# Negated upper parts and an adding DMA in place of VectorE's subtraction, for the second layer's weight blocks

## The chip, the cores and the metric

One Trainium2 chip, one core, one launch. The metric is the device time of the launch in microseconds (us). A second, finer source is one profiled execution: its span runs from the first to the last instruction, and the trace behind it says which engine did what and what it waited for. Engines are named as the profile names them: PE (TensorE matmul), DVE (VectorE), ACT (ScalarE), POOL (GpSimd), SP (SyncE, which here only issues DMAs). A q behind an engine's name (SPq) is its queue of DMA issues.

## The reference, cut to what matters

Two layers over x of shape (4, 512, 256), all float32. Layer 0 is a small recurrent mixer, gated; layer 1 is causal attention, gated. Both gates are the same kind of feed-forward network, and the second one's weights are what the change touches:

```python
xn = layernorm(x)
s  = attention(xn)                 # layer 1; a mixer in layer 0
up_gate = xn @ W1.T                # (.., 1024)
up_lin  = xn @ W3.T
hidden  = fwht(silu(up_gate) * up_lin)
g  = silu(hidden @ W2.T)
x  = x + s * g
```

## The kernel before, in words

**Parts of a number.** PE multiplies in a reduced format (float32r), so each float32 matrix goes into PE as two parts: an upper part, the value rounded to that format, and a lower part, the value less its upper part. A product is three matmuls: upper by upper, upper by lower, lower by upper. The helper `split` (line 59) makes the parts: ACT copies with rounding (L61), DVE subtracts (L62). Both lines stand for very many tiles, so the profile is read by tile name.

**Layer 0** works a batch (512 rows) at a time, b = 0 to 3, in `ffn`. Its matmuls are named f_b: `f_3gu` are the up products of batch 3, `f_3dn` the down products. Over eight chunks c of 128 hidden columns it makes two up products (gate and linear), a silu on ACT (L523), their product on DVE (L524), the split of that product (`f_3hh` on ACT, `f_3hl` on DVE), and then, a chunk later, the down products, which take `f_3hh` and `f_3hl` as weights. The up products have three PSUM banks for two per chunk: the second up product of chunk c+1 needs the silu of chunk c to have read its bank, and the first of chunk c+2 needs the gating product L524 of chunk c.

**Layer 1** uses a Strassen-like scheme in `ffn_s`: each 512-wide quarter q of the weights is cut into four blocks of 256 columns, and four sums of blocks are added, seven blocks in all. Blocks and sums are made once, while layer 0 runs batches 2 and 3, by `prep_s(q)` (L322): SP loads four raw blocks into `sraw` (L325), DVE forms four sums in `ssum` (L330 to L333), and both are split into `sp` tiles (three of the raw blocks, 128x768; four sums, 128x1024), which SP stores to DRAM (L342). In layer 1, `load_s` (L345, issue at L350) loads both parts of a quarter (`sw`, 896 KB each) anew for every batch. `sw` tiles share four buffers with layer 0's weights (tag `w13`), so the first ones are loaded while batch 3 of layer 0 finishes with those, each behind its PE wait.

**Side work in layer 0.** `Beside` hands steps of generators to slots between the chunks: for b = 2 the mixer, `prep_s(0)`, the norm of batch 3, `prep_s(1)`, the layer-1 norm of batch 0, `prep_s(2)`; for b = 3 the mixer, the first attention's transposes and splits, `prep_s(3)`. The number beside a generator (4 for `prep_s`) says how many steps it counts for.

**What decides the order.** The kernel is written against a scheduling layer (`TileContext`). It takes the traced program, orders each engine's instructions by its own timing model, gives tiles their buffers, and puts in the semaphore waits. Every engine and every DMA queue then works strictly in the built order: what stands behind a waiting instruction waits too. From layer 0's last products on, PE's order is written out by hand instead. Most tiles of 4 KB per partition, `sraw`, `ssum`, `sp`, and the attention's tiles among them, share ten buffers (tag `t4`), so a tile that is kept longer pushes others to other buffers.

**Names used below.** `ln_3r`, `ln_0r`, `mr`, `ssr`: row scales, raised to the power -1/2 by POOL (L261, L277, L724), its only regular work. `xn_3`: the normed batch 3 of layer 0. `mrb`: mean and scale rows of layer 1's norm, broadcast through DRAM by SP (L445, L447). `osb`: the mixer's output. `tsum`, `tb`, `xf`, `xg`: layer 1's activations for batch 0, made from two transposes. `tq`, `v`, `sc`: products of the attention.

Of the kernel before, what the change touches and what calls it, by code (L numbers as in the profile page):

```python
# [11 lines left out]
F32 = mybir.dt.float32  # L12
# [3 lines left out]
F32R = mybir.dt.float32r  # L16
AF = mybir.ActivationFunctionType
ALU = mybir.AluOpType
# [3 lines left out]
P = 128  # L22
D = 256
# [12 lines left out]
def kernel(ctx: ExitStack, tc: tile.TileContext, a: dict, out: bass.AP):  # L36
    nc = tc.nc
# [6 lines left out]
    def t4(name, shape, dt=F32):  # L44
        return act.tile(shape, dt, tag="t4", name=name, bufs=10)
# [10 lines left out]
    def psum(name, shape, tag="ms", bufs=3):  # L56
        return ps.tile(shape, F32, tag=tag, name=name, bufs=bufs)

    def split(src, hi, lo, engine=nc.vector):

        h = nc.scalar.copy(hi, src)  # L61
        return h, engine.tensor_tensor(lo, src, hi.bitcast(F32), ALU.subtract)  # L62
# [14 lines left out]
    def transpose(*args):  # L77
        return in_line(nc.tensor.transpose, *args)
# [94 lines left out]
    def w2_tile(name):  # L173
        return wp.tile([P, NH, D], F32R, tag="w2", name=name, bufs=4)

    def w2_tiles(layer):
        return w2_tile(f"w2h_{layer}"), w2_tile(f"w2l_{layer}")
# [73 lines left out]
    def moments(name, x, mr):  # L251

        st = act.tile([P, NT, 6], F32, tag="stats", name=f"{name}st", bufs=4)
        mv = act.tile([P, NT, 2], F32, tag="mv", name=f"{name}mv", bufs=4)
        for t in range(NT):
            nc.vector.bn_stats(st[:, t, :], x[:, t, :])
        for t in range(NT):
            nc.vector.bn_aggr(mv[:, t, :], st[:, t, :])
        nc.vector.tensor_copy(mr[:, 0, :], mv[:, :, 0])
        first["moments"] = nc.vector.tensor_scalar(mr[:, 1, :], mv[:, :, 1], LN_EPS, None, ALU.add)  # L260
        nc.gpsimd.tensor_tensor(mr[:, 1, :], mr[:, 1, :], mhalf, ALU.pow)  # L261

    def layernorm(name, x, y, groups=(NT,)):

        t0 = 0
        for i, n in enumerate(groups):
            ts_ = range(t0, t0 + n)
            st = act.tile([P, NT, 6], F32, tag="stats", name=f"{name}st{i}", bufs=4)
            mv = act.tile([P, NT, 2], F32, tag="mv", name=f"{name}mv{i}", bufs=4)
            r = small(f"{name}r{i}")  # L270
            for t in ts_:
                nc.vector.bn_stats(st[:, t, :], x[:, t, :])
            for t in ts_:
                nc.vector.bn_aggr(mv[:, t, :], st[:, t, :])
            rs = r[:, t0 : t0 + n]
            nc.vector.tensor_scalar(rs, mv[:, t0 : t0 + n, 1], LN_EPS, None, ALU.add)
            nc.gpsimd.tensor_tensor(rs, rs, mhalf[:, :n], ALU.pow)  # L277
            for t in ts_:
                ins = nc.vector.tensor_scalar(
                    y[:, t, :], x[:, t, :], mv[:, t, 0:1], r[:, t : t + 1], ALU.subtract, ALU.mult  # L280
                )
            t0 += n
        return ins

    def transpose_half(name, y, k):
        o = psum(f"{name}tp{k}", [P, S])
        for t in range(NT):
            transpose(o[:, sl(t)], y[:, t, sl(k)], ident)
        return o
# [14 lines left out]
    def xt_pair(name):  # L304

        both = act.tile([P, 2, 2, S], F32R, tag="xt", name=name, bufs=2)
        return both[:, 0], both[:, 1]
# [14 lines left out]
    def prep_s(q):  # L322

        raw = t4(f"sraw{q}", [P, 4, D])
        nc.sync.dma_start(raw, a["w13_1"][q])  # L325
        yield
        sums = t4(f"ssum{q}", [P, 4, D])
        a11, a12, a22, a21 = (raw[:, i, :] for i in range(4))
        s1, s2, s3, s4 = (sums[:, i, :] for i in range(4))
        nc.vector.tensor_tensor(s1, a21, a22, ALU.add)  # L330
        nc.vector.tensor_tensor(s3, a11, a21, ALU.subtract)
        nc.vector.tensor_tensor(s2, s1, a11, ALU.subtract)
        nc.vector.tensor_tensor(s4, a12, s2, ALU.subtract)  # L333
        yield
        sdram[q] = there = [
            dram.tile([P, 7, D], F32, tag=f"s{i}", name=f"s{i}_{q}", bufs=4) for i in range(2)
        ]
        for at, n, src in ((0, 3, raw), (3, 4, sums)):
            parts = [t4(f"sp{at}_{i}_{q}", [P, n, D], F32R) for i in range(2)]
            split(src[:, :n, :], *parts)  # L340
            for i in range(2):
                nc.sync.dma_start(there[i][:, at : at + n, :], parts[i].bitcast(F32))  # L342
            yield

    def load_s(q, n):  # L345
        parts = [
            wp.tile([P, 7, D], F32R, tag="w13", name=f"sw{i}_{n}_{q}", bufs=4) for i in range(2)
        ]
        for i in range(2):
            nc.sync.dma_start(parts[i].bitcast(F32), sdram[q][i])  # L350
        return parts
# [75 lines left out]
    def norm(layer, b):  # L427
        xn = act.tile([P, NT, D], F32, tag="xn", name=f"xn{layer}_{b}", bufs=3)
        xns[layer, b] = xn
        with after(first["gate"] if b > 1 - layer else None):  # L430
            first["scaled"] = layernorm(f"ln{layer}_{b}", xs[b], xn)
        yield
        if layer:


            mr = act.tile([P, 2, NT], F32, tag="mr", name=f"mr{b}", bufs=2)
            moments(f"ln2_{b}", xn, mr)
            yield
            o = psum(f"mrp{b}", [2 * NT, P], **DN[b == 0])
            transpose(o, mr.rearrange("p a t -> p (a t)"), ident)  # L440
            rows = act.tile([2 * NT, P], F32, tag="rows", name=f"rows{b}", bufs=1)
            with after(first["table"] if b else None):
                nc.scalar.copy(rows, o)
            there = dram.tile([2 * NT, P], F32, tag="rows", name=f"there{b}")
            nc.sync.dma_start(there, rows)  # L445
            mrb = t4(f"mrb{b}", [P, 2, S])
            nc.sync.dma_start(  # L447
                mrb, there.rearrange("(a t) p -> a (t p)", a=2).unsqueeze(0).to_broadcast([P, 2, S])
            )
            mrs[b] = mrb  # L450
            yield
            return
        hi, lo = xTs[0, b] = xt_pair(f"xt0_{b}")
        for k in range(2):
            o = transpose_half(f"xt0_{b}", xn, k)
            split(o, hi[:, k, :], lo[:, k, :])
            yield

    def after(ins):
        return tc.issue_after(ins.ins) if ins else nullcontext()  # L460
# [441 lines left out]
    def run(f, *args):  # L902
        return lambda: f(*args)

    def call(f, *args):
        f(*args)
        yield


    NORM, MIXER, W2P = 3, 3, 12  # L910
# [80 lines left out]
    for b in range(B):  # L991
        tasks = []
        if b == 0:
            prep = prep_first()
            next(prep)
            tasks.append((prep, 11))
        if b:
            tasks.append((call(gate_all, f"g0_{b - 1}", dn, xns[0, b - 1], xs[b - 1]), 1))
        tasks.append((mixer(b), MIXER))
        if b + 1 < B:  # L1000
            if b:
                load_x(b + 1)
            if b == 2:
                tasks.append((prep_s(0), 4))
            tasks.append((norm(0, b + 1), NORM))
        if b == 0:
            early = w2_tile("early0"), w2_tile("early1")
            spare = [
                [early[i][:, 2 * c : 2 * c + 2, :].rearrange("p a d -> p (a d)") for i in range(2)]
                for c in range(NH // 2)  # L1010
            ]
        if b == 1:
            raw2_1 = load_w2(1)
            w2_1 = w2_tiles(1)
            tasks.append((prep_w2(1, raw2_1, w2_1, t4), W2P))
            tasks.append((prep_second(), 5))
        if b == 2:
            tasks += [(prep_s(1), 4), (norm(1, 0), NORM), (prep_s(2), 4)]
        if b == 3:
            atts = [Attention(0)]  # L1020
            at = atts[0]
            parts = run(at.xt_half, 0), run(at.xt_half, 1), at.xt, at.scaled, at.split_sums
            tasks += [(call(f), 1) for f in parts]
            norms = {1: norm(1, 1)}
            tasks.append((prep_s(3), 4))
        bg = Beside(*tasks)
        if b == 0:
            dn = ffn("f0_0", xTs[0, 0], w13, w2, bg.slot, NH, spare, parts=2, behind=True)
        else:
            tail = [run(atts[0].tq, j) for j in range(2)] if b + 1 == B else []  # L1030
            dn = ffn(f"f0_{b}", xTs[0, b], w13, w2, bg.slot, tail=tail)
        bg.finish()
# [148 lines left out]
```

## Time and profile before

| | |
|---|---|
| median of 3 runs | 362.86 us (362.65 to 363.22) |
| the profiled execution's own time | 362.72 us |
| its span | 360.9 us |
| granted TensorE clock | 1.00 |
| DVE, ACT, POOL busy | 286.1, 197.5, 19.0 us (79%, 55%, 5%) |
| DMA of the kernel's own queues | q1 39.8%, q10 0.2% of 16 engines' span |

Busy time is the time in which an engine worked on an instruction of the program. A PE row of many matmuls is pipelined: a matmul of 512 columns is listed with some 0.39 us, but in an unbroken run the next starts 0.23 us later (0.12 us after one of 256 columns), so starts are compared, not durations. The same holds in a smaller way for DVE and ACT: a DVE operation over 512 columns is listed with 0.68 us and the next starts 0.60 us later.

### The profile page before, as it was taken

The page shows a single profiled execution, that of the slowest core. Times are in us where ns is not written, and L with a number is a line of the kernel's source. Part 1 is how long each engine was busy: PE and PEld are TensorE (multiplying, and loading weights), DVE is VectorE, ACT ScalarE, POOL GpSimd, SP SyncE. Part 2 cuts the span into 40 slices and gives each one's busy share as a digit, 9 for nine tenths or more (in the row PEclk, how much of TensorE's full clock was granted, in tenths as well). Part 3 has the DMA queues.
Part 4 walks back from the last instruction along what each step waited for, and adds up shares of the span by engine and source line. Part 5 has one row for each costly group of instructions (what it writes and reads, how often), then busy time and mean ns, then how long its engine had stood idle before and what let it go on. Part 6 is the DMA issues. An engine that isn't in the chain of part 4 may idle for free.

```text
span 360.9 us, 6262 instructions
## 1 busy us (share of the span) xinstructions
PE 354.3 (98%) x2469; PEld 327.9 (91%) x2469; DVE 286.1 (79%) x592; ACT 197.5 (55%) x372; POOL 19.0 (5%) x22
## 2 busy tenths in 40 slices
PE   8999999999999999999999999999999999999995
PEld 6878999888988898888999999999999999999995
DVE  6897868996679938898987957989679888568646
ACT  4665436274454335465467655576555676446443
POOL 1000201100011000100100001100011000000000
PEclk9999999999999999999999999999999999999999
DMA  7935000301063217637257135661554635345401
GB/s 228 346 108 186 3 0 2 116 0 60 0 196 155 118 52 236 237 130 254 85 206 261 49 157 205 223 226 79 203 205 152 215 162 203 136 149 193 194 2 58
DMA packets 16284, 52.25 MB, mean 145 GB/s; under 512 B 1632, under 2 KB 7936, under 8 KB 16256
## 3 DMA queue, kind: packets, MB, share of 16 engines
q1 hardware_dynamic: 15968, 51.60, 39.8%
q8 instruction: 19, 0.31, 0.3%
q10 hardware_dynamic: 288, 0.26, 0.2%
q14 instruction: 9, 0.07, 0.1%
HBM read 42.40 MB, written 9.45 MB: 144 GB/s over the span
## 4 chain that ended last, share of the span: by engine, by line
PE 78%; DVE 16%; ACT 2%; DMA 1%; issue 1%; POOL 1%; DVEq 0%; SPq 0%; ACTq 0%
PE f_0gu L70 6%; PE f_1gu L70 6%; PE f_0dn L70 5%; PE f_2dn L70 5%; PE f_3dn L70 5%; PE f_1dn L70 5%; PE f_3gu L70 5%; PE pv L70 4%; PE f_2gu L70 3%; PE tq L70 2%; PE o L70 2%; PE v L70 2%; PE sc L70 2%; PE warm L70 2%; DMA sraw<-in_w 1%; DVE sp L62 1%
## 5 line engine op out<-in xcount | busy, mean ns | idle before, releaser
L70 PE MATMUL f_3gu<-xt,w 128*128 128x512 f32 x96 | 25.6, 397 | 0.0
L70 PE MATMUL f_0gu<-xt,w 128*128 128x512 f32 (+1 forms) x108 | 24.9, 382 | 0.0
L70 PE MATMUL f_1gu<-xt,w 128*128 128x512 f32 x96 | 24.8, 395 | 0.0
L70 PE MATMUL f_2gu<-xt,w 128*128 128x512 f32 x96 | 24.6, 395 | 0.0
L70 PEld LDWEIGHTS f_0gu<-xt,w 128*128 128x128 f32 x108 | 18.6, 188 | 4.4 <-issue 1.0
L70 PEld LDWEIGHTS f_2gu<-xt,w 128*128 128x128 f32 x96 | 17.2, 188 | 3.2
L70 PEld LDWEIGHTS f_1gu<-xt,w 128*128 128x128 f32 x96 | 17.1, 188 | 3.2
L70 PEld LDWEIGHTS f_3gu<-xt,w 128*128 128x128 f32 x96 | 17.1, 188 | 2.9
L61 ACT CAST f_1hh<-f_1h 128x512 fp32r<-128x512 f32 x16 | 10.0, 623 | 16.7 <-DVE f_1h L524 13.6
L70 PE MATMUL f_1dn<-w2l,f_1hh 128*128 128x256 f32 x64 | 17.8, 282 | 0.0
L70 PE MATMUL f_2dn<-w2h,f_2hh 128*128 128x256 f32 x64 | 17.8, 283 | 0.0
L70 PE MATMUL f_1dn<-w2h,f_1hh 128*128 128x256 f32 x64 | 17.8, 281 | 0.0
L70 PE MATMUL f_2dn<-w2l,f_2hh 128*128 128x256 f32 x64 | 17.7, 283 | 0.0
L70 PE MATMUL f_3dn<-w2l,f_3hh 128*128 128x256 f32 x64 | 17.7, 282 | 0.0
L70 PE MATMUL f_3dn<-w2h,f_3hh 128*128 128x256 f32 x64 | 17.7, 281 | 0.0
L70 PE MATMUL f_3dn<-w2h,f_3hl 128*128 128x256 f32 x64 | 17.0, 283 | 0.4 <-DVE f_3hl L62 0.4
L70 PE MATMUL f_1dn<-w2h,f_1hl 128*128 128x256 f32 x64 | 17.1, 283 | 0.0
L70 PE MATMUL f_2dn<-w2h,f_2hl 128*128 128x256 f32 x64 | 16.8, 283 | 0.2 <-DVE f_2hl L62 0.2
L61 ACT CAST f_2hh<-f_2h 128x512 fp32r<-128x512 f32 x16 | 9.9, 621 | 12.4 <-DVE f_2h L524 9.1
L61 ACT CAST f_3hh<-f_3h 128x512 fp32r<-128x512 f32 (+1 forms) x17 | 10.1, 596 | 11.3 <-DVE f_3h L524 7.1
L62 DVE TENSOR_TENSOR f_2hl<-f_2h,f_2hh 128x512 fp32r<-128x512 f32 x16 | 10.9, 682 | 3.9 <-ACT f_2hh L61 3.8
L70 PE MATMUL f_0dn<-w2h,f_0hl 128*128 128x256 f32 x48 | 13.7, 284 | 0.1
(480 smaller groups left out, 1139.4 us busy)
## 6 DMA issues: line engine op xcount, KB each, us to landing
sw<-s SPq DMA_DIRECT2D x32, 896.0 KB, 5.5
s<-sp SPq DMA_DIRECT2D x8, 512.0 KB, 4.1
s<-sp SPq DMA_DIRECT2D x8, 384.0 KB, 2.5
w2raw<-in_w SPq DMA_DIRECT2D x4, 512.0 KB, 5.9
sraw<-in_w SPq DMA_DIRECT2D x4, 512.0 KB, 4.4
mrb<-there SPq DMA_DIRECT2D x4, 512.0 KB, 3.9
w13raw<-in_w SPq DMA_DIRECT2D x3, 512.0 KB, 6.6
x<-in_x SPq DMA_DIRECT2D x3, 512.0 KB, 3.4
```

The source lines that it names most:

```text
L61: h = nc.scalar.copy(hi, src)
L62: return h, engine.tensor_tensor(lo, src, hi.bitcast(F32), ALU.subtract)
L70: ins = call(*args, **kwargs)
```

## The change

Step by step, for the raw blocks and for the sums of each quarter: ACT makes the negated upper part (a multiplication by -1 with rounding) and then the upper part; a DMA issued by POOL adds the negated upper part onto the float32 source in place, which leaves the lower part there; SP stores the upper part as before, and the source itself as the lower part. The subtraction on DVE is gone. `prep_s` has one step more, and counts as 5.

```diff
+
         for at, n, src in ((0, 3, raw), (3, 4, sums)):
-            parts = [t4(f"sp{at}_{i}_{q}", [P, n, D], F32R) for i in range(2)]
-            split(src[:, :n, :], *parts)
-            for i in range(2):
-                nc.sync.dma_start(there[i][:, at : at + n, :], parts[i].bitcast(F32))
+            src = src[:, :n, :]
+            hi, neg = (t4(f"sp{at}_{i}_{q}", [P, n, D], F32R) for i in range(2))
+            nc.scalar.mul(neg, src, -1.0)
+            nc.scalar.copy(hi, src)
+            nc.gpsimd.dma_start(src, neg.bitcast(F32), accum_op=ALU.add)
+            nc.sync.dma_start(there[0][:, at : at + n, :], hi.bitcast(F32))
             yield
+            nc.sync.dma_start(there[1][:, at : at + n, :], src)
+        yield
...
-                tasks.append((prep_s(0), 4))
+                tasks.append((prep_s(0), 5))
...
-            tasks += [(prep_s(1), 4), (norm(1, 0), NORM), (prep_s(2), 4)]
+            tasks += [(prep_s(1), 5), (norm(1, 0), NORM), (prep_s(2), 5)]
...
-            tasks.append((prep_s(3), 4))
+            tasks.append((prep_s(3), 5))
```

Since the layer orders the program anew, other instructions of batches 2 and 3 change places too; the listing of both built programs shows which.

## The prediction

> **What bounds the kernel now.** I read the page's first part, then what PE waited for, then PE's and DVE's order of time around each wait, then DVE's and ACT's rows of the tiles that change.
>
> ```profile
> PE 354.3 (98%) x2469; PEld 327.9 (91%) x2469; DVE 286.1 (79%) x592; ACT 197.5 (55%) x372; POOL 19.0 (5%) x22
> ```
>
> PE is the bound, with 6.6 us of idle span. What it waited for, by the waits view:
>
> ```profile
> PE warm L70 <- DVE zr L921: 1.4, 1, 1.4
> PE f_3dn L70 <- DVE f_3hl L62: 0.4, 1, 0.4
> PE f_2dn L70 <- DVE f_2hl L62: 0.2, 1, 0.2
> ```
>
> (Us in total, times, longest.) The first is the start. The other two lie in the stages that the change touches, one each in batches 2 and 3. PE's order of time shows their price:
>
> ```profile
> 112.44 1.55 PE L70 MATMUL f_2gu<-xt,w 128*128 128x512 f32 x6
> 114.22 0.38 PE L70 MATMUL f_2dn<-w2h,f_2hl 128*128 128x256 f32 x1 [0.22 <-DVE f_2hl L62]
> 114.44 0.28 PE L70 MATMUL f_2dn<-w2h,f_2hh 128*128 128x256 f32 x1
> ...
> 170.57 0.28 PE L70 MATMUL f_3dn<-w2l,f_3hh 128*128 128x256 f32 x1
> 171.27 0.39 PE L70 MATMUL f_3dn<-w2h,f_3hl 128*128 128x256 f32 x1 [0.42 <-DVE f_3hl L62]
> 171.50 0.28 PE L70 MATMUL f_3dn<-w2h,f_3hh 128*128 128x256 f32 x1
> ```
>
> Six up matmuls take 1.39 us from start to start, so the product of 114.22 was due at 113.83: 0.39 lost, and 0.10 more since its successor follows after 0.22 instead of 0.12. The second was due at 170.69: 0.58 and 0.11. Together **1.18 us**; elsewhere between 94 and 171 us no PE row shows idle time. DVE at those two places:
>
> ```profile
> 112.51 0.92 DVE L62 TENSOR_TENSOR sp<-sraw,sp 128x768 fp32r<-128x768 f32 x1
> ...
> 113.51 0.66 DVE L62 TENSOR_TENSOR f_2hl<-f_2h,f_2hh 128x512 fp32r<-128x512 f32 x1
> ...
> 168.68 1.20 DVE L62 TENSOR_TENSOR sp<-ssum,sp 128x1024 fp32r<-128x1024 f32 x1
> 169.81 0.68 DVE L62 TENSOR_TENSOR tql<-tq,tqh 128x512 fp32r<-128x512 f32 x1
> ...
> 170.56 0.65 DVE L62 TENSOR_TENSOR f_3hl<-f_3h,f_3hh 128x512 fp32r<-128x512 f32 x1
> ```
>
> In both, a subtraction of `sp` stands ahead of the late `f_2hl` or `f_3hl`. The change removes exactly these.
>
> **What goes.** Eight DVE subtractions: 4 x 0.95 + 4 x 1.22 = 8.7 us (rows of `sp`). Beside PE's 98% all of it but the two waits is hidden, so the ceiling of the gain is 1.18 us. Without the 1.13 us that `sp` occupies, the second `f_3hl` starts near 169.4 and ends before 170.2, ahead of 170.69; its upper part is ready at 168.1. The first is freed likewise: in the built order nothing of `prep_s` stands between the row sums of `ln_3` and `f_2hl` but one block sum (0.34), and my sum of DVE's starts puts `f_2hl`'s end at 113.0.
>
> **What comes on ACT.** Eight copies with a factor of -1. A factor costs ACT nothing visible: 0.60 us for `wqkh` (factor, 128x512) against 0.58 for `tqh` (copy). So 4 x 0.84 + 4 x 1.05 = 7.6 us, on an engine at 55%. Behind them on ACT are silu and upper part of the next chunks. In batch 2 the tightest is the silu of chunk 2: it ends near 106.9, and PE needs it at 108.24. In batch 3 both copies of `sraw` go ahead of chunk 1's silu (139.3, wanted at 142.4). Cover: over 1 us; price here nothing. Without that cover each further copy would cost PE up to its 0.74 to 0.96 us.
>
> **What comes on POOL.** Eight DMA issues, which the trace does not have. Queued behind them are `ln_3r`, `ln_0r`, `mr` and `ssr`. An adding DMA waits for ACT's copy of the same tile and DVE's last block sum. `ln_3r` stands behind the third one (ready near 112.3); `xn_3` is then done near 116.8, and PE's transposes want it near 119. For an issue I take SPq's 0.3 to 0.6 us as the lower bound, and as the upper one POOL's own 1.0 to 1.4 us for an operation; even two of the latter fit into the 2.2 us. Nothing.
>
> **How long an adding DMA takes.** No row shows it. Below: a plain copy of the same 512 KB (`s<-sp`), 4.1 us median. Above: twice the longest landing of `s<-sp`, 6.6, so 13.2 us. The page *Collectives: The Full Stack*, section "The bandwidth ceiling", says that an add in the DMA path reads two sources and so runs at half a copy's rate. The row alone would give 4, the rule 8; I take **8 us**, since the stretch from 140 to 148 us already moves 263 to 422 GB/s and the adds fall into it.
>
> A second rule speaks against the change: *SBUF — State Buffer*, section "SBUF: two separate sides", warns that POOL cannot write a DMA's descriptors while DVE runs an operation that takes both port pairs, as a float32 copy in SBUF does; its example grows from 620 to 3100 ns. The nearest such rows here, `xn<-x` (TENSOR_SCALAR, 128x256), start 0.33 us apart, as two-input additions do (0.34): no double rate, hence no sign of that mode. By the row nothing is added; by the rule's example 2.5 us are, and 8 becomes 10.5.
>
> **What comes on SP.** The store of the lower part now waits for the add, and SP keeps its order. Behind the one of `ssum` for q = 2 stand the load of `sw`'s lower half and of `sraw` for q = 3. ACT makes that negated part near 141.5 and the upper part near 142.5, so with 8 us the add lands near 150.6. The lower half of `sw` may not go before PE is done with its buffer, now 149.19, so SP is held some 1.4 us. `sraw` for q = 3 is issued near 151.4 instead of 158.48, as it moved ahead of another `sw`; with its 5.4 us it lands near 156.8. DVE's block sums for q = 3 moved forward too, behind chunk 4's gating product, near 157.9. So nothing waits, with **1 us of slack**: that is the point at which the adds begin to cost. The `sw` behind `sraw` q = 3's store would be issued near 168 instead of 165.5, and is wanted at 182. The longer hold on the ten buffers costs nothing more, as no reuse in the built order comes that close.
>
> **What is moved.** With DVE's subtractions gone the order is made anew, and in batch 3 DVE gets more to do before chunk 4's gating product. Now `ssr` of the mixer is at 147.59 and that product ends at 154.88. In the built order, between the same two: three 256-column operations (0.34 apart), four of `osb` (1.6), seven of 512 (0.60), two of 1024 (1.13), then the product (0.60 + 0.69 for the two gating ones): 1.0 + 1.6 + 4.2 + 2.3 + 1.3 = 10.4 us. `ssr` itself comes at about 147.5, as ACT's extra copies for q = 2 (0.74 + 0.96) use what is now waiting time. So the product ends near 157.9. PE wants it for the up product of chunk 6: now at 157.87, then 157.38, the first gap being closed. **A new wait of 0.5 us, with the slower start 0.6.** Both of its bounds: below, nothing (my sums of starts are good to about 0.6); above, 1.2.
>
> **Sum**, against the profiled execution's own 362.72 us: -0.49 - 0.69 + 0.6 = -0.6, 362.1. The median of the runs is 0.14 above that execution: **362.3 us**.
>
> **The rivals.**
> 1. *Gaps closed, one new wait on DVE* (as above): 362.3, between 361.7 and 362.9. Chance 0.42.
> 2. *The new wait doesn't arise*, DVE and PE fitting as the scheduler intended: 362.86 - 1.18 = 361.7. For it: PE has 3 us of slack at that product now. Against: the sum of 10.4 us. Chance 0.21.
> 3. *The add holds SP.* Slower. From 9 us of an add on, `sraw` for q = 3 lands late, and DVE waits in its block sums with chunk 4's lower part and chunk 5's gating product queued behind. At 13 us it lands at 161.9, 4 us late; PE has some 0.8 us of slack there (chunk 4's lower part ready near 160.4, wanted near 161.2). That is +3.2 on top of rival 1: 365.5. For it: DMA traffic in that stretch, two reads per add, a wait on SP that did not exist. Against: 13 is my upper bound. Chance 0.27.
> 4. *The gaps only move*: freed DVE time goes to row statistics that were ordered forward, and PE meets the same wait elsewhere: 362.9. Against: DVE loses 3% of its work. Chance 0.10.
>
> **How the numbers follow.** About 0.2% (0.73 us, so 362.13 and 363.59) is what a measurement tells from no change. Faster by more: 0.21 of rival 2 and 0.12 of rival 1, 0.33. Within: 0.28 of rival 1, 0.07 of rival 4, 0.35. Slower: 0.27 of rival 3, the rest of 1 and 4, 0.32. The range leaves out the slowest third of rival 3 and little below 361.5: 361.5 to 366.0. The likeliest case's own is 361.7 to 362.9.
>
> **What would show it.** Right: no PE wait for `f_2hl` and `f_3hl` near 114 and 170, DVE busy near 277 us, ACT near 205, and one PE wait of about half a microsecond for `f_3h` L524's successor near 157. Rival 3: DVE idle for the DMA of `sraw` near 158, and an issue to landing of the adds above 9 us. Rival 2: PE idle down by 1.2 us with no new wait. Wrong altogether: POOL rows of several microseconds per DMA issue, with `xn_3` late, or waits in layer 1, which I take to be unchanged.

## The result, and the profile after

The changed kernel takes **363.97 us** (median of 13 runs, 363.35 to 364.89) against 362.92 (362.65 to 363.22) of the kernel before beside it: ratio 1.0027, 95% interval 1.0019 to 1.0036. It is slower by 1.05 us where I forecast 0.6 us less. The profiled execution took 363.47 us with a span of 361.3.

The page's first part, the row of the engines:

```profile
PE 354.0 (98%) x2469; PEld 328.2 (91%) x2469; DVE 278.5 (77%) x584; ACT 204.1 (56%) x380; POOL 25.9 (7%) x30
```

The work went where it was meant to go: DVE is down by 7.6 us, ACT up by 6.6, POOL up by 6.9 for eight issues. What PE waited for (us in total, times, longest):

```profile
PE warm L70 <- DVE zr L926: 1.5, 1, 1.5
PE f_3dn L70 <- ACT f_3hh L61: 1.1, 1, 1.1
PE f_0dn L70 <- DVE f_0hl L62: 0.2, 1, 0.2
```

Both old waits, behind `f_2hl` and `f_3hl`, are gone. In their place stands one behind an upper part, which ACT makes. PE's order of time there:

```profile
157.35 0.28 PE L70 MATMUL f_3dn<-w2h,f_3hl 128*128 128x256 f32 x1
157.69 1.68 PE L70 MATMUL f_3gu<-xt,w 128*128 128x512 f32 x6
160.44 0.38 PE L70 MATMUL f_3dn<-w2h,f_3hh 128*128 128x256 f32 x1 [1.08 <-ACT f_3hh L61]
160.66 0.28 PE L70 MATMUL f_3dn<-w2l,f_3hh 128*128 128x256 f32 x1
```

From start to start: 157.69 comes 0.34 after its predecessor instead of 0.12 and its own six are 0.10 slow, 0.32 together: DVE's gating product, which I had at 0.6. Then 160.44 comes 2.75 after 157.69 instead of 1.39, or 1.25 after the slow start is taken off, and 0.10 more follow: **1.35 us behind `f_3hh`**, which is in no step of my sum. So PE's starts say -1.18 + 0.32 + 1.35 = +0.49. The span grew by 0.4, and the time outside the span from 1.82 to 2.17 us (see the end).

What made `f_3hh` late is read from the chain of work that ends with it (start, us, what):

```profile
142.97 7.75 DMA ssum<-sp
...
150.77 0.32 SPq L347
...
151.15 0.42 SPq L355
...
151.62 6.05 DMA sraw<-in_w
...
157.78 0.85 ACT sp L342
158.63 0.72 ACT sp L343
159.35 0.52 ACT xgh L61
159.87 0.53 ACT f_3hh L61
...
160.44 0.74 PE f_3dn L70 x4
```

Read downwards: the add of `ssum` q=2 lands; SP may then store the lower part, load a `sw` and, third, load the raw blocks of q=3; ACT, which had been free since 156.15 (its row shows 1.63 us idle before the copy), waits for them with the negated copy at its head; two copies and `xgh` later it makes `f_3hh` of chunk 4, for which PE has been waiting.

**Theory 1:** the add holds the last chunk's load, and that load holds ACT, with `f_3hh` queued behind. **Rivals:** the new order and ACT's extra 7.6 us cost the time whatever the load does; or the adds cost it wherever they run, by traffic, by their number or outside the span.

### The profile page after: what moved, and what is told of

The parts are those of the page before. It is cut to its first block, busy times and chain, and to the rows that moved or that the text cites. A ratio compares the mean times of both kernels' runs of the same rounds, so it can differ in the third digit from the quotient of the medians.

```text
span 361.3 us, 6295 instructions
## 1 busy us (share of the span) xinstructions
PE 354.0 (98%) x2469; PEld 328.2 (91%) x2469; DVE 278.5 (77%) x584; ACT 204.1 (56%) x380; POOL 25.9 (7%) x30
## 4 chain that ended last, share of the span: by engine, by line
PE 78%; DVE 11%; DMA 6%; ACT 3%; issue 1%; POOL 1%; SPq 0%; DVEq 0%; ACTq 0%
PE f_0gu L70 6%; PE f_1gu L70 6%; PE f_2gu L70 6%; PE f_0dn L70 5%; PE f_2dn L70 5%; PE f_1dn L70 5%; PE f_3dn L70 4%; PE pv L70 4%; PE tq L70 3%; DMA sraw<-in_w 3%; PE o L70 2%; PE v L70 2%; DMA ssum<-sp 2%; PE sc L70 2%; PE f_3gu L70 2%; PE warm L70 2%
## 5 line engine op out<-in xcount | busy, mean ns | idle before, releaser
L70 PE MATMUL f_3gu<-xt,w 128*128 128x512 f32 x96 | 24.7, 397 | 0.1
L62 DVE TENSOR_TENSOR f_3hl<-f_3h,f_3hh 128x512 fp32r<-128x512 f32 (+1 forms) x17 | 11.1, 656 | 5.1 <-ACT f_3hh L61 5.0
```

Source lines behind the costliest of these rows:

```text
L70: ins = call(*args, **kwargs)
```

## The experiments

In each group the kernel before ran on the same chip: 362.83 us for the first four, 363.17 for the next four, 363.05 for the last three. I tell them in the order of the argument.

**No add at all** (2nd group)

```diff
-            nc.gpsimd.dma_start(src, neg.bitcast(F32), accum_op=ALU.add)
```

> The changed kernel without the adding DMAs: the subtraction is left out, and what is stored as the lower part is the source itself; ACT's negated copies, all loads and all stores stay. It has the order of ACT of the changed kernel around `f_3hh` of chunk 4, but no load, store or buffer waits for an add. Theory 1 (what costs is the time of the adds, which hold buffers and so the load): `sraw` of q=3 is issued by 146, ACT doesn't wait for it, DVE's short wait of 0.3 us may stay, and the time is 361.8 to 362.4. Rival (the moved order on ACT and DVE and ACT's 7.6 us more of work cost the time): the wait behind `f_3hh` of about 1 us stays and the time is 363.5 to 364.

Measured: 361.49 us, ratio 0.9955 (0.9942 to 0.9969), some 0.3 below theory 1's range. ACT's order of time:

```profile
154.98 0.85 ACT L342 ACTIVATE sp<-sraw 128x768 fp32r<-128x768 f32 x1 [2.37 <-DMA sraw<-in_w]
155.74 0.82 ACT L343 CAST sp<-sraw 128x768 fp32r<-128x768 f32 x1
156.86 0.82 ACT L774 ACTIVATE xg<-xf,gb 128x512 f32<-128x512 f32 x1 [0.30 <-DVE xf L772]
157.58 0.60 ACT L61 CAST f_3hh<-f_3h 128x512 fp32r<-128x512 f32 x1
```

The two copies stand ahead of `f_3hh` as in the changed kernel, and ACT even waits longer for the load; but the load was issued at 149.57 and landed 2.8 us earlier, so `f_3hh` starts at 157.58 instead of 159.77, and PE loses 0.12 us there. I expected the issue by 146; `sw`, in front of it on SP, waits for PE until 149.20, adds or not. With the load on time this order of ACT costs next to nothing, so the order alone is not the cost: the loss needs the late load.

**Chunk q=2 the old way** (2nd group)

```diff
+        if not (q != 2):
+            for at, n, src in ((0, 3, raw), (3, 4, sums)):
+                parts = [t4(f"sp{at}_{i}_{q}", [P, n, D], F32R) for i in range(2)]
+                split(src[:, :n, :], *parts)
...
+            return
```

> The changed kernel with chunk q=2 alone split the old way (DVE subtracts, its lower part is a tile of its own), adds for q=0, 1 and 3. Theory 1 (the load of `sraw` q=3 waited for the buffer that the add of `ssum` q=2 held): the load is issued near 145 instead of 151.6, ACT's wait at it and PE's 1.35 us behind `f_3hh` go; one of the two old waits (behind an `sp` subtraction of q=2, about 0.5) may come back: 362.4 to 363.0. Rival (q=3's own adds, or the number of adds, cost the time): 363.6 to 364.

Measured: 361.48 us, ratio 0.9954 (0.9941 to 0.9966), better than expected, as neither old wait came back: the load is issued at 149.72 (not near 145, for `sw` again stands in front of it until 149.35), and PE waits for nothing but the start:

```profile
PE warm L70 <- DVE zr L934: 1.5, 1, 1.5
```

Six of the eight adds are still there, those of q=3 among them, and cost nothing that shows. But this edit moves two things: the new build also has `f_3hh` of chunk 4 ahead of the two copies on ACT.

```profile
155.78 0.61 ACT L61 CAST f_3hh<-f_3h 128x512 fp32r<-128x512 f32 x1
157.30 0.83 ACT L350 ACTIVATE sp<-sraw 128x768 fp32r<-128x768 f32 x1
```

So the earlier load and the changed order are not told apart here; the run without adds, which keeps the copies in front, does that.

**Chunk q=3 the old way** (3rd group; the edit of the last run with another condition)

```diff
-        if not (q != 2):
+        if not (q < 3):
```

> The changed kernel with the last chunk (q=3) split the old way, adds for q=0, 1 and 2: the counterpart to the run with q=2 undone. Theory 1 (the harm comes from q=2's add, ahead of the load, and from ACT's copies of q=3's raw blocks ahead of `f_3hh` of chunk 4, not from q=3's own adds): the load is issued near 151.6 as in the changed kernel and lands near 157; ACT waits for it, with one copy of 0.73 us fewer behind the wait, so PE still loses 0.4 to 1.2 us near 160: 363.0 to 363.8. Rival (q=3's own adds cost the time): the wait goes and the time is as with q=2 undone, 361.4 to 361.8.

Measured: 362.98 us, ratio 0.9994 (0.9986 to 1.0003), just below theory 1's range, and not to be told from the kernel before. PE's wait is there though q=3 has no add:

```profile
160.10 0.39 PE L70 MATMUL f_3dn<-w2h,f_3hh 128*128 128x256 f32 x1 [0.53 <-ACT f_3hh L61]
```

The load was issued at 151.78 and ACT's one copy started at 158.18; PE lost 0.80 us. The two runs together clear q=3's own adds: without them the wait stays, and with them it is absent once q=2's adds are gone.

**The changed kernel again** (3rd group, nothing edited)

> The changed kernel once more, unaltered, beside the two others on the same chip. Theory 1: 363.8 to 364.4 us, with the wait of 1.0 to 1.5 us behind `f_3hh` near 160 and the same time outside the span, 2.1 to 2.2 us, since that has been the same in every run of one program so far. If the loss were of the chip of the first measurement, it would be within 0.2 us of the kernel before.

Measured: 364.44 us, ratio 1.0048 (1.0029 to 1.0066), a shade above theory 1's range. In its profile the load took 6.54 us, ACT's copy started at 158.33, and PE lost 1.94 us. Against the first profile the copy came 0.55 later and the loss was 0.59 larger; against the run before this one there is one copy more (0.75 us) and the start is 0.15 later, PE's up products begin 0.26 earlier (157.66 against 157.92), and the loss is 1.14 larger. The loss follows the start of the copies nearly one to one. It fits that the first 13 runs of this kernel spread over 1.5 us where those of the kernel before spread over 0.6: here a DMA's landing is on PE's path.

One thing is not explained by the landing. Three of the eight runs took 365.83 to 366.35 us, and their mean granted TensorE clock was 0.995; the other five took 363.59 to 364.70 at 0.998 to 1.000, and none of the first 13 runs was below 0.997. A mean of 0.995 over 364 us is 1.8 us of full clock, about what sets the three apart (an estimate). No trace shows one of these three; two traces below show the clock at 0.50 for some microseconds behind a wait of PE.

**Is it SP's order or the buffer?** (3rd group)

```diff
-            nc.sync.dma_start(there[1][:, at : at + n, :], src)
+            eng = nc.gpsimd if q == 2 and at else nc.sync
+            eng.dma_start(there[1][:, at : at + n, :], src)
```

> The changed kernel with one store moved to another queue: the lower part of `ssum` q=2, which waits for the add of that tile and stood on SP ahead of the last chunk's raw load, is issued by POOL, behind the add itself. SP isn't held any more; the load's buffer, though, is still the tile that this add reads. It asks which of the two holds the load. Theory 1a (SP's order alone): the load of `sraw` q=3 is issued at 149.6 as in the kernel without adds, lands by 155.2, and PE's 1.35 us behind `f_3hh` shrink to 0.2: 362.6 to 363.0 us. Theory 1b (the buffer holds it as well): the load is issued when the add has landed, 150.5 to 151, lands near 156.3 to 157, PE loses 0.5 to 1.1 us, and the time is 363.2 to 363.8.

Measured: 363.97 us, ratio 1.0037 (1.0022 to 1.0052). SP's order of time, what the load waited for, and ACT's order of time:

```profile
149.36 0.32 SPq L356 DMA_DIRECT2D sw<-s  x1
150.97 0.33 SPq L325 DMA_DIRECT2D sraw<-in_w  x1
```

```profile
SPq L325 <- DMA ssum<-sp: 1.3, 1, 1.3
```

```profile
158.24 0.85 ACT L342 ACTIVATE sp<-sraw 128x768 fp32r<-128x768 f32 x1 [1.86 <-DMA s<-ssum]
```

SP is past `sw` at 149.68 and free, yet the load starts at 150.97, when the add has landed: in the built program its buffer is the negated tile that this add reads. Theory 1b holds for the issue. The time is over its 363.8, for a reason that I had not foreseen: the negated copy of q=3 takes the buffer of the tile that is being stored, and the store now ends last (6.9 us), so PE lost 1.59 us. Freeing one queue moved the wait to another buffer.

**Each add twice** (1st group; each of half the negated part)

```diff
-            nc.scalar.mul(neg, src, -1.0)
+            nc.scalar.mul(neg, src, -0.5)
...
-            nc.gpsimd.dma_start(src, neg.bitcast(F32), accum_op=ALU.add)
+            for _ in range(2):
+                nc.gpsimd.dma_start(src, neg.bitcast(F32), accum_op=ALU.add)
```

> The changed kernel, with each adding DMA made twice, each time of half the negated part (so the sum is the same), one behind the other: what waits for the sum waits for two adds, some 5 to 7 us longer. Theory 1 (the add of `ssum` q=2 frees the buffer late, SP issues the load of q=3's raw blocks behind it, ACT waits for that load): the load is issued near 157 to 158 and lands near 163, ACT's wait grows from 1.6 to some 7 us, PE's wait behind `f_3hh` from 1.35 to 6 to 7 us, and the time is 369 to 371. Rival (the latency of the add is not what counts, but the order on ACT and DVE): the time stays within 1 us of 364.0.

Measured: 373.37 us, ratio 1.0290 (1.0275 to 1.0304), 2 us above theory 1's range. PE's waits, and the chain:

```profile
PE f_3dn L70 <- DVE f_3hl L62: 5.4, 1, 5.4
PE f_3gu L70 <- DVE f_3h L530: 2.3, 2, 1.4
```

```profile
144.19 5.24 DMA sraw<-sp
...
149.72 6.29 DMA sraw<-sp
156.02 4.78 DMA s<-sraw
160.82 6.05 DMA sraw<-in_w
...
166.99 0.43 DVE ssum L330
167.42 0.34 DVE ssum L331
167.75 0.61 DVE f_3hl L62
168.41 2.07 PE f_3dn L70 x8
```

The late load is again what PE waits for in the end, but it holds another reader. In this build ACT made `f_3hh` of chunk 4 at 160.87, before it stood at the load (5.40 us idle); DVE stood at the load with its block sums, and `f_3hl` behind them kept PE waiting. The issue missed, too: 160.82 instead of 157 to 158, since here the load waited for the store behind the two adds as well. The rival, that the latency does not count, is out.

The wait of 5.4 us is no longer than forecast. What goes beyond the range is 2.3 us at gating products, earlier in the batch, and a slower PE behind the long wait:

```profile
168.41 0.58 PE L70 MATMUL f_3dn<-w2h,f_3hl 128*128 128x256 f32 x1 [5.39 <-DVE f_3hl L62]
...
170.28 4.58 PE L70 MATMUL f_3gu<-xt,w 128*128 128x512 f32 x12
174.70 0.28 PE L70 MATMUL f_3dn<-w2h,f_3hh 128*128 128x256 f32 x1
```

Twelve up matmuls take 4.42 us from start to start instead of 2.8, and the granted clock was 0.50 between 168 and 172 us, where the changed kernel has 1.00 throughout. From 168.41 to 174.70 that is 6.29 us for what takes 3.7 at the usual spacing: 2.6 us lost.

**The load early** (2nd group)

```diff
         if b == 3:
+            last_s = prep_s(3)
+            next(last_s)
...
-            tasks.append((prep_s(3), 5))
+            tasks.append((last_s, 4))
```

> The changed kernel, with the load of the last chunk's raw blocks (`sraw` of q=3) asked for at the start of batch 3, ahead of that batch's other tasks, so that it takes a buffer that no late adding DMA holds. The adds, the copies and their number stay. Theory 1 (the 1.35 us are ACT at a load that the add of `ssum` q=2 had held up): the load is issued before 145 and landed before 152, ACT's wait and PE's wait behind `f_3hh` near 160 go, and the time is 362.4 to 362.9 us. Rival from the first runs (ten buffers and longer holds: take the wait away in one place and another instruction waits for an add's buffer): a new wait behind an `sp` DMA of 1 us or more appears later, and the time is 363.7 or more.

Measured: 361.69 us, ratio 0.9960 (0.9948 to 0.9973), a little better than expected. The load is issued at 139.98; PE waits only at the start (1.5 us). All eight adds are in place, and 512 KB take 7.0 us by the median, longer than in the changed kernel (6.5). So the adds as such are not the cost. As with q=2 undone, `f_3hh` of chunk 4 (155.37) now stands ahead of the copies of q=3 (157.60) on ACT, so this run too moves the load and the order together.

**The negated copy later** (1st group)

```diff
-            nc.scalar.mul(neg, src, -1.0)
+            with after(first["hh"] if q == 3 and at == 0 else None):
+                nc.scalar.mul(neg, src, -1.0)
```

> The changed kernel, with one order of ACT altered: the negated copy of the last chunk's raw blocks (the `sp` from `sraw` of q=3) must come behind the `f_hh` that stands newest when it is recorded, so ACT no longer waits for that load with `f_3hh` of chunk 4 behind it. Theory 1 (the loss is ACT standing at a late load, 1.35 us of PE behind `f_3hh`): that wait of `f_3dn` at 160.4 goes, DVE's short wait of 0.3 us stays, and the time is 362.6 us, some 1.3 below the changed kernel and 0.3 below the kernel before. Rival (the adding DMAs slow things wherever they run, the wait is only where it shows): the wait moves to another product of the same batch, and the time stays within 0.3 us of 364.0.

Measured: 366.98 us, ratio 1.0106 (1.0083 to 1.0129). The half of theory 1 that it asks about held: PE's `f_3dn` at 159.68 comes 1.51 us after its predecessor, no wait, though the load is as late as in the changed kernel (issued at 152.19; DVE waits for it until 158.59). So it takes both, a late load and ACT's copies in front of `f_3hh`. But the copy ended up behind the last chunks, at 164.02 instead of 157.78, so q=3's add was issued at 165.88, took 9.57 us, and DVE's order of time says who stood behind it:

```profile
176.00 1.29 DVE L62 TENSOR_TENSOR tql<-tq,tqh 128x512 fp32r<-128x512 f32 x2 [4.90 <-DMA sraw<-sp]
```

```profile
PE f_0gu0g L70 <- DVE f_0h L657: 1.7, 1, 1.7
PE v L70 <- DVE tql L62: 1.5, 1, 1.5
```

(The second fence shows PE's waits.) `tql` had to wait for the add to let a buffer go. The expectation of 362.6 was wrong by 4.4 us: I had moved the add along with the copy and not asked who needs its tiles. The rival's "the wait moves" is what happened, only into another stage and larger. Here, too, the clock fell behind a wait: 0.50 between 186 and 188 us. Of the six runs, the two with a mean clock of 0.997 and 1.000 took 365.3 us, the four with 0.995 took 366.6 to 367.8.

**The gain without an add** (1st group; the splits of the kernel before, held behind the newest `f_hl`)

```diff
-            split(src[:, :n, :], *parts)
+            with after(first["hl"]):
+                split(src[:, :n, :], *parts)
```

> The kernel before, no adding DMA: only the splits of the weight blocks (the rounded copies of ACT and the subtractions of DVE) must come behind the `f_hl` that is newest when they are recorded. Theory 1 (the two waits of PE in the kernel before, 0.49 and 0.69 us, are the place of the `sp` subtractions ahead of `f_2hl` and `f_3hl` on DVE): both waits go without taking the subtractions off DVE, and the time is 361.7 to 362.3. Rival (the load of DVE matters, not the place): the waits move to other products, and the time is 362.7 to 363.2.

Measured: 361.82 us, ratio 0.9972 (0.9962 to 0.9983). Both old waits are gone with DVE still at 285.7 us. So they were a matter of place, not of DVE's load. New ones of 0.6 and 0.2 us (`f_0gu1z` and `f_0gu2z` behind DVE's `f_0h`) take back part of the 1.18.

**The subtractions on POOL** (2nd group)

```diff
-            split(src[:, :n, :], *parts)
+            split(src[:, :n, :], *parts, engine=nc.gpsimd)
```

> The kernel before with the eight `sp` subtractions moved from DVE to POOL as they are: no adding DMA, no negated copy, the lower part a tile of its own. It asks what taking the subtractions off DVE is worth without the adds' latency and holds. Theory 1: both old waits of PE (0.49 and 0.69 us) go, the 128x768 and 128x1024 subtractions take POOL 2 to 4 us each with slack enough, and the time is 361.7 to 362.3. Rival (POOL and DVE get in each other's way, so DVE's instructions beside POOL's grow longer; or the stores come too late): 362.8 to 364.

Measured: 363.39 us, ratio 1.0007 (0.9998 to 1.0015): the rival. A POOL row and a DVE row of the same moment:

```profile
165.54 2.40 POOL L62 TENSOR_TENSOR sp<-ssum,sp 128x1024 fp32r<-128x1024 f32 x1 [3.66 <-ACT sp L61]
```

```profile
166.01 2.47 DVE L62 TENSOR_TENSOR f_3hl<-f_3h,f_3hh 128x512 fp32r<-128x512 f32 x1 [1.04 <-ACT f_3hh L61]
```

An `f_3hl` that takes 0.68 us elsewhere takes 2.47: it ends when POOL's subtraction has ended (167.94) and its own time is over. One `xn` of 0.41 us took 2.50 in the same way. The wait behind `f_3hl` is gone, but in batch 2 PE now waits for gating products that DVE makes late:

```profile
PE f_2gu L70 <- DVE f_2h L524: 0.4, 2, 0.3
```

The work left DVE and came back as stalls: the spans are 361.0 to 361.7 us against 361.1 to 361.7 of the kernel before.

**One adding DMA that nobody waits for** (1st group, kernel before)

```diff
+    idle = [small(f"idle{i}") for i in range(2)]
+    for t in idle:
+        nc.gpsimd.memset(t, 0.0)
+    nc.gpsimd.dma_start(idle[0], idle[1], accum_op=ALU.add)
```

> The kernel before, with two small tiles (128x4) set to zero and one adding DMA between them on POOL's queue near the start, which nobody waits for. Theory 1 says that 0.35 us of the loss lies outside the span and comes with any use of POOL's software queue: the execution's time less its span goes from 1.82 to about 2.17 us, the span stays within 0.2 of 360.9, and the time is 363.2 to 363.3. Rival (the 0.35 us is the end of the changed program, or chance): time less span stays at 1.8 and the time at 362.9.

Measured: 362.55 us, ratio 0.9991 (0.9983 to 0.9999), time outside the span 1.74 to 1.85 us. My explanation of the 0.35 us falls.

## Why the prediction was wrong, step by step

- **The ceiling of 1.18 us** was right: both waits went, and kernels that add no other wait gain it in the profile (span 359.7 with q=2 undone, 360.9 before).
- **The add's 8 us** were right: 7.75 us for the one that mattered, landing at 150.7 against 150.6; by the median 6.5 us for 512 KB against 3.8 for the plain copy `s<-sp` of the same kernel, 1.7 times. How much of that is the adding and how much POOL's queue is not shown: the one plain store that POOL issued (in "Is it SP's order or the buffer?") took 6.9 us, beside the load. POOL's issues took 0.86 to 1.04 us, with no sign in these rows of the 2.5 us that I had worked out from the example in the Trainium skill, page *SBUF — State Buffer*, section "SBUF: two separate sides".
- **POOL's queue** cost nothing, as I said: `ln_3r` at 114.22, no wait of PE near 119.
- **The new DVE wait** was 0.32 us, not 0.6, within its bounds.
- **The step that failed** is the one on SP: "So nothing waits, with 1 us of slack". The issue was as forecast (151.62 against 151.4), the load took 6.05 us instead of 5.4, and it landed 0.9 us later than I said. That alone was inside the slack. But the slack was that of the wrong waiter: I had asked when DVE's block sums come (157.9; they did wait 0.17), and not ACT's negated copy, which the built order has at ACT's head from 156.15, with `xgh`, `f_3hh` and a silu behind it. With the load at 156.8 as forecast, PE would still have lost 1.35 - 0.9, some 0.45 us (an estimate).
- **ACT's "price here nothing"** failed with it: I checked the copies of q=1 and q=2 against the silu behind them, and not those of q=3 against `f_3hh`. The added copy of q=3 is 0.75 us of the 1.35.
- **"The longer hold on the ten buffers costs nothing more"** was wrong: the buffer of `sraw` q=3 is one that the add still reads, and in three experiments a tile waited for an add or a store behind it.
- **Rival 3** had the mechanism, "the add holds SP", but its threshold ("from 9 us of an add on"), its waiter (DVE) and its price (+3.2) were off. It decided at less than 8 us, by ACT. With each add made twice, DVE is the waiter as the rival has it: 5.4 us behind its block sums.

With -1.18 + 0.32 + 1.35 in place of my -1.18 + 0.6, the sum on the profiled execution is 363.2; the rest to 363.47 lies outside the span. Since the landing varies, the typical loss is larger: the second profile of the same program shows 1.94.

Two versions beat both kernels by repairing that one load: q=2 split the old way (361.48 us) and the load early (361.69), some 0.4 to 0.5% below the kernel before. Simply moving the subtractions, with no add, gets 361.82; that one ran in another group, and the intervals overlap in part. The first two ran side by side with spans of 359.6 to 359.8 us each; the 0.2 us between them lies outside the span. So I don't rank the three.

## What to carry to other kernels

When an operation with a long latency replaces a short one, follow its landing through everything that is issued or allocated behind it, and for the last load in that line list *every* engine that reads it, with what is queued behind each reader: the slack is that of the earliest reader. A tile that a DMA still reads is a held buffer, and a cure that delays the DMA moves the hold. If a wait is due to an instruction's place, try its place first: here that gave most of the gain for no new latency.

## What I had not expected of the hardware

- Beside a POOL subtraction that reads two tiles (1.85 to 2.55 us), some DVE operations stand still: 0.68 us became 2.47 (two inputs) and 0.41 became 2.50 (`xn`, one input and two scalars). Three BATCH_NORM_STATS2 (one input) beside another such subtraction, near 112 us, kept their 0.41 us. The Trainium skill, page *SBUF — State Buffer*, section "Who interferes with whom", says that a DVE instruction with two inputs in SBUF contends with a POOL instruction that reads SBUF; the `f_3hl` row agrees, and it stood until POOL's instruction had ended. For a TENSOR_SCALAR such as `xn` the section expects this only in a mode that takes both port pairs. The prediction saw no sign of that mode in the rows of `xn`, yet this one stood still; why stays open.
- Behind a wait the granted clock can fall to half: 0.50 between 168 and 172 us after PE's 5.4 us (each add twice), 0.50 between 186 and 188 us after 1.7 us (the negated copy later). What decides it is not shown: in the second profile of the changed kernel a wait of 1.7 us had no such stretch behind it.
- The time outside the span is a constant of each program: 1.73 to 1.87 us in the runs of the kernel before and of six experiments, 2.10 to 2.21 in the changed kernel and three others, 1.97 to 2.04 in one. It doesn't go with the adds: the kernel with sixteen of them has 1.74 to 1.79, the one with POOL's subtractions and none has 2.12 to 2.19. What sets it stays open, and with it 0.35 of the 1.05 us.
